# Grouping layer 1's 16-bit and 32-bit products by pairs of block groups

## The chip, the cores and the metric

The kernel runs on one core of a Trainium2 chip. A core has five engines that work side by side, each through its own queue in order: TensorE (PE, matrix products into PSUM), VectorE (DVE), ScalarE (ACT), GpSimd (POOL) and SyncE (SP, which here only issues DMA transfers). The metric is device time in microseconds (us) for one execution, and less is better.

## The reference, cut to what matters

The program is a graph network of four layers over 2708 nodes with 128 features. Its adjacency matrix `adj` is 2708 x 2708, about 0.6% filled plus the diagonal. Every layer normalises its input, applies relu, computes an update and adds it to x. The change touches layer 1 alone, a layer of messages:

```python
s = node_feats @ msg_w[:, :D].T
d = node_feats @ msg_w[:, D:].T
messages = gelu(s[:, None, :] + d[None, :, :] + msg_b)
aggregated = einsum('ijd,ij->id', messages, adj)
new_feats = concatenate([node_feats, aggregated]) @ upd_w.T + upd_b
h = gelu(new_feats) + node_feats          # then a layer norm
```

A message is needed only where `adj[i, j]` is not zero. The kernel therefore lists the non-zero entries of every row first (in layer 0's stage) and computes messages for listed entries only. Layer 0 is a weighted mean over neighbours, layer 2 a gated recurrent cell, layer 3 an attention with two heads.

## The kernel before

**Stages.** From the start of the profiled span to about 215 us the kernel reads `adj`, lists its entries and computes layer 0. Layer 1's set-up runs to about 273 us and its loop from there to 606 us; a tail of small operations follows. Layers 2 and 3 fill the rest.

**Tiles and blocks.** The 2708 rows make 22 tiles of 128 (the last has 20). The columns make 22 blocks of 124 (the last has 104). Six groups of up to four blocks (`GB` = 6) are handled one after another: groups 0 to 4 have four blocks, group 5 has two. For one tile t and one block there are up to 128 listed entries ("slots").

**One period for one tile.** `period(t)` runs for t = 0 to 22. Within it a loop over k = 0 to 5 issues, for the present tile, and for tiles further up and down the pipeline:

- `combine(t, k)` (L620, L624): for each block of group k, six 16-bit (bf16) products into one PSUM tile `p_m`. Three pick the rows' part s (split into three bf16 pieces) by the 0/1 matrix `sel`, three pick the columns' part d by `cols`. This makes s + d for every slot.
- `activate(t, k)` (L632): gelu on ScalarE, from `p_m` to a tile `g` (named `g1`) in SBUF.
- `gather(t, k)` (L645): for each block one 32-bit product of `g` with `put`, which holds the adjacency values at their rows. A 32-bit product shows as two weight loads and two matmuls in the profile (x8 for four blocks). They add up in `agg`. Group k is gathered two steps after it was combined; groups 4 and 5 are gathered in steps 0 and 1 of the next period.
- `close_tile(t - 1)` (L653): the diagonal entries of the tile before are added in 32 bits; after each fourth tile `agg` is copied to `aggT`.
- `pass_on(t + 1)` (L560 to L567): column numbers of the next tile are turned on TensorE (`p_w`), copied out by ScalarE (`where_T`), and sent through DRAM to all partitions (`spread`).
- `rank(t + 3)` (L465 to L467): a 16-bit product `p_r`, and two VectorE copies of it, `ends` and `ends4`.
- `fetch(t + 2, half)` (L498): eleven 16-bit products `y`, and ScalarE copies of them (`lead`, `line`).
- `describe(t + 3)` (L418 to L420, and L474 on POOL): the listed values of a tile split into three bf16 pieces (`xb`), by ScalarE, VectorE, ScalarE and POOL in turn.
- `sources(k)` (L588 to L607), in even periods up to 18: two 32-bit products `p_s` for the next pair of tiles, a VectorE addition (`sb`, L595), and then a split like that of `describe` (`s`, `s_r`), a gelu and two scalings on ScalarE.
- `update(g, 0)` (L679, L680), in periods 5, 9, 13, 17 and 21 inside the loop: eight 32-bit products `p_u` for a group of four tiles, and a VectorE addition. Steps 1 to 7 of `update` follow one period apart each; they are layer 1's gelu, its layer norm and the next layer's norm.
- `select_rows`, `count_rows`, `columns` (L574), `place`, `finish_rows` (L487), `list_late` (L459, L461): VectorE work that prepares `sel`, `cols` and `value` for later tiles. `finish_rows` also waits for a DMA.
- `put_values` (POOL) and `put_more` (ScalarE, L552): make `put`.

**What sets the order.** The loop stands inside `tc.manual_schedule()`. Each engine gets its instructions in the order in which the Python code calls them, and takes them in that order. A tile's buffer can be written again only when the readers of its former content are done. Three pools matter here: `p_m` has two PSUM buffers (`l1m`), `g1` has three buffers (`l1b`), and `p_w`, `p_r`, `p_s` and `p_u` all share the one PSUM bank of `rpool` (tag "r"). So each of these four waits until the one before it has been copied out.

Of the kernel before, what the change touches and what calls it, by code (L numbers as in the profile page):

```python
# [20 lines left out]
F32 = mybir.dt.float32  # L21
# [9 lines left out]
P = 128  # L31
N = 2708
D = 128
# [3 lines left out]
CH = 512  # L37
# [14 lines left out]
def size(t):  # L52
    return min(P, N - t * P)
# [7 lines left out]
def listed_layers(ctx: ExitStack, tc: tile.TileContext, x, adj, w, out, flag):  # L61
# [333 lines left out]
    with (  # L395
# [177 lines left out]
            st["cols"] = work.tile([P, NB, E], BF16, name="cols")  # L573
            nc.vector.tensor_scalar(st["cols"], st.pop("spread"), part, None, ALU.is_equal)  # L574

        own_rows, aggs = {}, {}

        def sources(k):

            p = rpool.tile([P, CH], F32, tag="r", name="p_s")  # L580
            pv = p.rearrange("p (t c d) -> p t c d", t=2, c=2)
            sb = once.tile([P, 2, 2, D], F32, name="sb")
            m = size(2 * k + 1)
            if m < P:
                nc.vector.memset(sb[:, 1, :, :], 0.0)
            for q in range(2):
                c, mq = (2 * k + q) * P, size(2 * k + q)
                nc.tensor.matmul(  # L588
                    p[0:mq, q * 2 * D : (q + 1) * 2 * D], hT[:, c : c + mq],
                    src_self.rearrange("p c d -> p (c d)"), start=True, stop=True,  # L590
                )
            bv = msg_b.unsqueeze(1).to_broadcast([P, 2, D])
            if m == P:
                bv = msg_b.unsqueeze(1).unsqueeze(1).to_broadcast([P, 2, 2, D])
                nc.vector.tensor_tensor(sb, pv, bv, ALU.add)  # L595
            else:
                for q in range(2):
                    mq = size(2 * k + q)
                    nc.vector.tensor_tensor(sb[0:mq, q, :, :], pv[0:mq, q, :, :], bv[0:mq, :, :], ALU.add)
            s3 = three.tile([P, 3, 2, D], BF16, name="s3")  # L600
            rest = once.tile([P, 2, D], F32, name="s_r")
            split([s3[:, q, :, :] for q in range(3)], sb[:, :, 0, :], rest)
            gs = three.tile([P, 2, D], F32, name="gs")
            nc.scalar.activation(gs, sb[:, :, 1, :], AF.Gelu)
            for q in range(2):
                t = 2 * k + q
                nc.scalar.activation(gs[:, q, :], gs[:, q, :], AF.Identity, scale=own[:, t : t + 1])  # L607
            own_rows[k] = s3, gs

        def combine(t, k):  # L610

            st = state[t]
            s3 = own_rows[t // 2][0]
            b0 = 4 * k
            n = min(4, NB - b0)
            p = mpool.tile([P, 4, D], F32, name="p_m")
            for b in range(b0, b0 + n):
                kb = width(b)
                for q in range(3):
                    nc.tensor.matmul(  # L620
                        p[:, b - b0, :], st["sel"][:, b, :], s3[:, q, t % 2, :], start=(q == 0), stop=False
                    )
                for q in range(3):
                    nc.tensor.matmul(  # L624
                        p[:, b - b0, :], st["cols"][0:kb, b, :], d3[0:kb, b, q, :], start=False, stop=(q == 2)
                    )
            st["p", k] = p

        def activate(t, k):
            n = min(4, NB - 4 * k)  # L630
            g = three.tile([P, 4, D], F32, name="g1")
            nc.scalar.activation(g[:, 0:n, :], state[t].pop(("p", k))[:, 0:n, :], AF.Gelu)  # L632
            state[t]["g", k] = g

        def gather(t, k):

            st = state[t]
            m = size(t)
            if k == 0 and t % 4 == 0:
                aggs[t // 4] = acc.tile([P, 4, P], F32, name="agg1")  # L640
            agg = aggs[t // 4][:, t % 4, 0:m]
            g = st.pop(("g", k))
            for b in range(4 * k, min(4 * k + 4, NB)):
                put = (st["put", 0][:, b, 0:m] if b < HP else st["put", 1][:, b - HP, 0:m])
                nc.tensor.matmul(agg, g[:, b - 4 * k, :], put, start=(b == 0), stop=False)  # L645
# [17 lines left out]


        STEPS = 8
        ups = {}

        def update(g, step):
            t, k = GROUPS[g]
            if step == 0:  # L670
                u = work.tile([P, 4, D], F32, name="u1")
                p = rpool.tile([P, CH], F32, tag="r", name="p_u")
                agg = aggs.pop(g)
                if size(t + k - 1) < P:
                    nc.vector.memset(u[:, k - 1, :], 0.0)
                for q in range(k):
                    m, c = size(t + q), (t + q) * P
                    pq = p[0:m, q * D : (q + 1) * D]
                    nc.tensor.matmul(pq, hT[:, c : c + m], upd_wT[:, 0, :], start=True, stop=False)  # L679
                    nc.tensor.matmul(pq, agg[:, q, 0:m], upd_wT[:, 1, :], start=False, stop=True)  # L680
                pv = p.rearrange("p (t d) -> p t d", t=4)
                bv = upd_b.unsqueeze(1).to_broadcast([P, 4, D])
                whole = k if size(t + k - 1) == P else k - 1
                nc.vector.tensor_tensor(u[:, 0:whole, :], pv[:, 0:whole, :], bv[:, 0:whole, :], ALU.add)
                if whole < k:
                    nc.vector.tensor_tensor(u[0:TAIL, whole, :], pv[0:TAIL, whole, :], upd_b[0:TAIL, :], ALU.add)
                ups[g] = [u]
            u = ups[g][0]
            rows = tiles_of(u, 0, k)
            if step == 1:  # L690
                nc.scalar.activation(u[:, 0:k, :], u[:, 0:k, :], AF.Gelu)
            if step == 2:
                nc.vector.tensor_tensor(u[:, 0:k, :], u[:, 0:k, :], h[:, t : t + k, :], ALU.add)
                ups[g].append(moments(rows, "n1u"))
            if step in (3, 6):
                ups[g].append(factors(*ups[g].pop()))
            if step == 4:
                scale_rows(rows, rows, *ups[g].pop(), AF.Identity)
                for v, op in ((ln_w, ALU.mult), (ln_b, ALU.add)):
                    nc.gpsimd.tensor_tensor(u[:, 0:k, :], u[:, 0:k, :], v.unsqueeze(1).to_broadcast([P, k, D]), op)  # L700
            if step == 5:
                nc.vector.tensor_tensor(xs[:, t : t + k, :], xs[:, t : t + k, :], u[:, 0:k, :], ALU.add)
                ups[g].append(moments(tiles_of(xs, t, k), "n2"))
            if step == 7:
                scale_rows(tiles_of(h, t, k), tiles_of(xs, t, k), *ups[g].pop(), AF.Relu)
                ups.pop(g)
# [10 lines left out]
        def period(t, between=()):  # L717

            now, c, b, a = (0 <= t + q < NT for q in range(4))
            last = 0 <= t - 1 < NT  # L720
            if c and not between:
                put_values(t + 1)
            for k in range(GB):
                for step in between[k : k + 1]:
                    step()
                if now:
                    combine(t, k)
                    activate(t, k)
                if k < 2:
                    if last:  # L730
                        gather(t - 1, GB - 2 + k)
                    if k == 0 and c:
                        pass_on(t + 1)
                    if k == 1 and last:
                        close_tile(t - 1)
                    if k == 1 and a:
                        rank(t + 3)
                elif now:
                    gather(t, k - 2)
                if k in (1, 2) and b:  # L740
                    fetch(t + 2, k - 1)
                if k == 1 and a:
                    describe(t + 3)
                if k == 2:
                    if now and t % 2 == 0 and t + 2 < NT:
                        sources(t // 2 + 1)
                    if a:
                        select_rows(t + 3)
                    if now and t + 4 < NT:
                        count_rows(t + 4)  # L750
                    updates(t)
                if k > 0 and c:
                    put_more(t + 1, k)
                if k == 3 and c:
                    columns(t + 1)
                if k == 3 and b:
                    place(t + 2)
                if k == 4 and a:
                    finish_rows(t + 3)
                if k == 4:  # L760
                    load_late(t + 1)
                if k == GB - 1:
                    list_late(t)
# [955 lines left out]
```

## Time and profile before

| What | us |
|---|---|
| Time, median of three runs (lowest to highest) | 1063.65 (1063.14 to 1064.64) |
| The profiled execution's own time | 1064.19 |
| Its span, from the first to the last instruction | 1062.3 |
| Layer 1's loop: first `combine` of tile 0 to last product of `close_tile(21)` | 273.5 to 606.1 |
| PE busy in the whole span | 931.0 (88%) |
| DVE busy | 816.0 (77%) |
| ACT busy | 516.6 (49%) |
| POOL busy | 450.6 (42%) |

The profile is one execution. A page gives busy times, forty slices of the span with busy tenths, and the costliest groups of instructions. The trace behind it answers for any stretch: which instruction ran when, what an engine was idle for, and what ended the idle time. "Period t" below runs from the first product of `combine(t, 0)` to that of `combine(t + 1, 0)`; times "in a period" count from its start. Matmuls overlap in the pipeline, so the distance between two starts is what a matmul costs the engine; its listed duration is longer.

### The profile page before, as it was taken

What the parts mean: (1) busy time and instruction counts of PE and PEld (TensorE: products, weight loads), DVE (VectorE), ACT (ScalarE), POOL (GpSimd) and SP (SyncE); (2) the same over time, 40 slices, a digit from 0 to 9 for tenths busy, and PEclk for the clock granted to TensorE, in tenths of its full rate; (3) what the DMA queues carried; (4) which work ended last, traced back from release to release, by engine and by line L of the source; (5) the groups of instructions that cost most, each with busy time, mean ns of one, the idle gap of its engine ahead of it and who ended that gap; (6) DMA issues with size and microseconds to landing.
All of it is one profiled execution on the core that took longest, in us unless ns stands there. A gap on an engine that the chain in (4) does not pass through costs nothing. (4 is left out here: it accounts for less than half of the span.)

```text
span 1062.3 us, 22020 instructions
## 1 busy us (share of the span) xinstructions
PE 931.0 (88%) x7950; PEld 751.1 (71%) x7950; DVE 816.0 (77%) x2853; ACT 516.6 (49%) x1450; POOL 450.6 (42%) x486
## 2 busy tenths in 40 slices
PE   5798789944799999999999969999979999989983
PEld 2454455433699999899899824444478899989982
DVE  7999999868577788787877264655578977997793
ACT  7777788534666666666666511433312200330142
POOL 3310112022798878787987172344320200250042
PEclk9999999756899999999999979999989999999996
DMA  9889997221233333322321155556410000000000
GB/s 364 312 301 323 308 359 253 74 67 45 80 108 118 125 99 104 106 92 83 108 87 58 65 201 180 199 192 217 124 38 21 12 4 1 2 16 6 1 11 19
DMA packets 60625, 129.67 MB, mean 122 GB/s; under 512 B 11160, under 2 KB 23828, under 8 KB 57798
## 3 DMA queue, kind: packets, MB, share of 16 engines
q1 hardware_dynamic: 58690, 125.38, 34.7%
q10 hardware_dynamic: 1816, 2.80, 0.9%
q8 instruction: 64, 1.05, 0.4%
q14 instruction: 55, 0.45, 0.1%
HBM read 81.55 MB, written 30.87 MB: 106 GB/s over the span
## 5 line engine op out<-in xcount | busy, mean ns | idle before, releaser
L543 POOL TENSOR_SCALAR put<-count,line,value 128x128 f32<-128x128 f32 x176 | 196.3, 1126 | 32.7 <-DVE value L532 24.4
L965 PE MATMUL att<-hv,wt 128*128 128x129 f32 x1672 | 195.5, 278 | 8.8 <-DVE wt L935 8.8
L965 PEld LDWEIGHTS att<-hv,wt 128*128 128x128 f32 x1672 | 191.8, 194 | 11.8 <-DVE wt L935 8.6
L620 PE MATMUL p_m<-s,sel 128*128 128x128 bf16 x1452 | 161.1, 219 | 6.6 <-ACT g L632 6.6
L624 PE MATMUL p_m<-d,cols 124*128 124x128 bf16 (+1 forms) x1452 | 161.4, 219 | 1.4 <-DVE cols L574 1.3
L121 POOL TENSOR_TENSOR n_r<-n_r,minus_half 128x4 f32<-128x4 f32 (+1 forms) x31 | 46.2, 1492 | 269.3 <-DVE n_r L120 263.7
L935 DVE SCALAR_TENSOR_TENSOR wt<-row,lift,mask 128x1024 f32<-128x1024 f32 (+1 forms) x132 | 138.1, 1075 | 25.0 <-PE att L965 25.0
L645 PE MATMUL agg<-put,g 128*128 128x128 f32 (+1 forms) x968 | 135.8, 281 | 0.0
L297 PE MATMUL acc<-a,hs 128*128 128x512 f32 (+2 forms) x264 | 123.9, 572 | 10.9 <-ACT hs L137 10.9
L1104 PE MATMUL p_agg<-a,hs 128*128 128x512 f32 (+2 forms) x264 | 111.7, 566 | 12.1 <-DMA a<-adjT 8.0
L309 PEld LDWEIGHTS p_T<-ident,a 128*128 128x128 f32 x484 | 59.6, 143 | 87.2 <-ACT aT L313 40.0
L645 PEld LDWEIGHTS agg<-put,g 128*128 128x128 f32 x968 | 118.1, 192 | 0.0
L620 PEld LDWEIGHTS <-sel 128*128 128x128 bf16 x1452 | 104.9, 97 | 10.9 <-issue 8.4
L285 DVE FIND_INDEX8 col<-val,a 128x8 uint16<-128x124 f32 (+1 forms) x400 | 106.2, 276 | 0.0
L309 PE MATMUL p_T<-ident,a 128*128 128x128 f32 x484 | 81.7, 287 | 25.3 <-ACT aT L313 19.6
L624 PEld LDWEIGHTS <-cols 124*128 124x128 bf16 (+1 forms) x1452 | 102.1, 97 | 1.9 <-DVE cols L574 1.9
L632 ACT ACTIVATE g<-p_m 128x512 f32<-128x512 f32 x132 | 73.0, 553 | 61.1 <-PE p_m L624 61.1
L552 ACT ACTIVATE put<-mine,value 128x128 f32<-128x128 bf16 x308 | 100.5, 390 | 0.0
L283 DVE MAX8 val<-a 128x8 f32<-128x124 f32 (+1 forms) x400 | 90.6, 266 | 2.8 <-DMA a<-in_adj 2.8
L313 ACT ACTIVATE aT<-p_T 128x512 f32<-128x512 f32 (+2 forms) x132 | 71.1, 541 | 43.9 <-ACT aT L313 33.2
L1104 PEld LDWEIGHTS p_agg<-a,hs 128*128 128x128 f32 (+1 forms) x264 | 48.4, 197 | 62.2 <-issue 52.0
L297 PEld LDWEIGHTS acc<-a,hs 128*128 128x128 f32 (+1 forms) x264 | 44.3, 201 | 26.2 <-issue 15.0
(261 smaller groups left out, 1504.1 us busy)
## 6 DMA issues: line engine op xcount, KB each, us to landing
a<-in_adj SPq DMA_DIRECT2D x21, 1354.0 KB
adjT<-aT SPq DMA_DIRECT2D x105, 256.0 KB
a<-adjT SPq DMA_DIRECT2D x20, 1280.0 KB
spread<-passed SPq DMA_DIRECT2D x22, 704.0 KB
later<-sel SPq DMA_DIRECT2D x22, 616.0 KB
row<-own_d ACTq DMA_DIRECT2D x10, 256.0 KB
later<-sel SPq DMA_DIRECT2D x22, 82.5 KB
adjT<-aT SPq DMA_DIRECT2D x21, 74.0 KB
```

The lines of the kernel that those rows point to most:

```text
L283: nc.vector.max(val[:, n, b, :], block(b))
L285: nc.vector.max_index(col[:, n, b, :], val[:, n, b, :], block(b))
L297: nc.tensor.matmul(accs[ci][:, 0:cw], h[0:m, n, :], sets[n // 4][0:m, n % 4, c : c + cw], start=(n == 0), stop=(n == NT - 1),)
L309: nc.tensor.transpose(p[0:k, q * P : q * P + m], sets[gi][0:m, q, j * P : j * P + k], ident[0:m, 0:m])
L543: nc.gpsimd.tensor_scalar(st["put", 0][:, b, :], count, st["line"][:, b : b + 1], st["value"][:, b : b + 1], ALU.is_equal, ALU.mult,)
L552: nc.scalar.activation(st["put", 1][:, b - HP, :], st["mine"][:, b - HP, :], AF.Identity, scale=st["value"][:, b : b + 1])
L620: nc.tensor.matmul(p[:, b - b0, :], st["sel"][:, b, :], s3[:, q, t % 2, :], start=(q == 0), stop=False)
L624: nc.tensor.matmul(p[:, b - b0, :], st["cols"][0:kb, b, :], d3[0:kb, b, q, :], start=False, stop=(q == 2))
L645: nc.tensor.matmul(agg, g[:, b - 4 * k, :], put, start=(b == 0), stop=False)
L935: nc.vector.scalar_tensor_tensor(wt[:, 0:n], row[:, k, c : c + n], lift[:, j, k : k + 1], mask[:, j, c : c + n], op0=ALU.max, op1=ALU.mult,)
L965: nc.tensor.matmul(banks[s // 3][:, s % 3, :], wt[:, q * P : (q + 1) * P], hv[:, j, k, :], start=(v < 2 and s // 3 not in touched), stop=( ...
L1104: nc.tensor.matmul(pa[:, 0:n], h[0:k, j, :], a[0:k, j - j0, 0:n], start=(j == 0), stop=(j == NT - 1))
```

## The change

Inside `period`, the order of the calls is new. `combine` still runs for k = 0 to 5. The gathers now come two at a time: those of groups 4 and 5 of the tile before in step 1, those of groups 0 and 1 in step 3, those of groups 2 and 3 in step 5. The first of each two stands after `combine(t, k)` and ahead of `activate(t, k)`, the second after `activate(t, k)`. `pass_on` moves ahead of `activate(t, 0)`, and `rank` ahead of both gathers of step 1.

The 32-bit products of `sources` and of `update`'s step 0 are taken out into two new functions, `project` and `mix`, which run in step 1 right after `close_tile`. Before, they stood in step 2. The work that reads them stays in step 2. No instruction is added or removed on any engine.

```diff
+        def project(k):
+
+            p = projected[k] = rpool.tile([P, CH], F32, tag="r", name="p_s")
             for q in range(2):
                 c, mq = (2 * k + q) * P, size(2 * k + q)
                 nc.tensor.matmul(
                     p[0:mq, q * 2 * D : (q + 1) * 2 * D], hT[:, c : c + mq],
                     src_self.rearrange("p c d -> p (c d)"), start=True, stop=True,
                 )
+
+        def sources(k):
+
+            if k not in projected:
+                project(k)
+            pv = projected.pop(k).rearrange("p (t c d) -> p t c d", t=2, c=2)
...
+        def mix(g):
+            t, k = GROUPS[g]
+            p = mixed[g] = rpool.tile([P, CH], F32, tag="r", name="p_u")
+            agg = aggs.pop(g)
+            for q in range(k):
+                m, c = size(t + q), (t + q) * P
+                pq = p[0:m, q * D : (q + 1) * D]
+                nc.tensor.matmul(pq, hT[:, c : c + m], upd_wT[:, 0, :], start=True, stop=False)
+                nc.tensor.matmul(pq, agg[:, q, 0:m], upd_wT[:, 1, :], start=False, stop=True)
...
                 if now:
                     combine(t, k)
+                if k == 0 and c:
+                    pass_on(t + 1)
+                if k == 1 and a:
+                    rank(t + 3)
+                if k == 1 and last:
+                    gather(t - 1, GB - 2)
+                elif k in (3, 5) and now:
+                    gather(t, k - 3)
+                if now:
                     activate(t, k)
-                if k < 2:
-                    if last:
-                        gather(t - 1, GB - 2 + k)
-                    if k == 0 and c:
-                        pass_on(t + 1)
-                    if k == 1 and last:
-                        close_tile(t - 1)
-                    if k == 1 and a:
-                        rank(t + 3)
-                elif now:
+                if k == 1 and last:
+                    gather(t - 1, GB - 1)
+                    close_tile(t - 1)
+                elif k in (3, 5) and now:
                     gather(t, k - 2)
+                if k == 1:
+                    if now and t % 2 == 0 and t + 2 < NT:
+                        project(t // 2 + 1)
+                    for g, (first, n) in enumerate(GROUPS):
+                        if t == first + n + 1:
+                            mix(g)
                 if k in (1, 2) and b:
                     fetch(t + 2, k - 1)
```

## The prediction

> **What bounds the kernel now.** I read the page's busy tenths first, to see which engine carries the stage that changes. Layer 1's loop is slices 10 to 22.
>
> ```profile
> PE   5798789944799999999999969999979999989983
> DVE  7999999868577788787877264655578977997793
> ACT  7777788534666666666666511433312200330142
> PEclk9999999756899999999999979999989999999996
> ```
>
> PE is at 9 and its clock at 9 through the loop, DVE at 7 and 8, ACT at 6. PE sets the pace, with DVE close behind. Next the list of waits, for PE alone, from 291.8 to 603.5 us (periods 1 to 21): whom PE waited for, us in total, times, longest.
>
> ```profile
> PE p_m L620 <- ACT g L632: 5.7, 7, 1.5
> PE y L498 <- DVE sel L487: 2.4, 5, 0.6
> PE p_m L624 <- DVE cols L574: 1.3, 2, 0.6
> ```
>
> So only 9.4 of 312 us are waits, of two kinds. In even periods `combine(t, 5)` waits for `activate(t, 3)`; in odd ones `fetch` or `combine` waits for DVE. Third, PE's timeline in period 8, for what a change of type costs.
>
> ```profile
> 402.05 0.33 PE L624 MATMUL p_m<-d,cols 124*128 124x128 bf16 x3
> 402.21 1.11 PE L645 MATMUL agg<-put,g 128*128 128x128 f32 x8
> 403.16 0.33 PE L620 MATMUL p_m<-s,sel 128*128 128x128 bf16 x3
> ```
>
> Eight 32-bit products hold PE for 0.95 us. Read one by one, the first holds it 0.165 and each other 0.1115; the bf16 ones around take 0.056 each. A bf16-to-f32 change thus costs 0.055 us. The way back costs nothing (0.112 from the last f32 start to the first bf16).
>
> **What the skill says.** The Trainium skill, "TensorE: Matmul & The Clock Gate", section "Weight-path perf modes", says that the fast weight load is off for FP32. The trace agrees: a bf16 load is listed with 96 to 100 ns, an f32 load with 192. The same page, "Architectural detail", says that PE alone pulls weight loads ahead, and that ScalarE and VectorE are strictly first in, first out. The waits above fit that. Its "Part 1: The HAM clock gate" gives free-running windows of 3413 ns, one idle window halving the clock. The record here changes clock at multiples of 3.41 us, and 265.3 to 275.5 us shows half clock released only after a full busy window. "Perfetto Trace Analysis", "Optimization Strategy", says that repeated bubbles can mean that buffers are short. The PSUM bank of `rpool` is such a place below.
>
> **Part 1: fewer changes of type.** Before, a period has 6 runs of f32 products, plus one for `p_s` in 10 even periods and one for `p_u` in 5 odd ones: 6 x 22 + 15 = 147. After, each period has 3, and what is left in period 22 joins the last of them: 66. Saved: 81 x 0.055 = 4.4 us. A period without waits falls from 13.53 us (period 7) to 13.37, an even one from 14.48 to 14.27, one with `mix` from 15.41 to 15.19.
>
> **Part 2: the even periods' chain on ACT.** This is the wait of `combine(t, 5)`. ACT's timeline of period 2 (start 305.33):
>
> ```profile
> 310.26 0.21 ACT L499 CAST lead<-y 128x55 bf16<-128x55 f32 x1 [0.36 <-PE y L498]
> 311.39 0.37 ACT L420 CAST xb<-v_r 128x176 bf16<-128x176 f32 x1 [0.60 <-DVE v_r L419]
> 312.24 0.57 ACT L632 ACTIVATE g<-p_m 128x512 f32<-128x512 f32 x1
> 314.52 0.41 ACT L418 CAST s<-sb 128x256 bf16<-128x256 f32 x1 [1.47 <-DVE sb L595]
> 315.41 0.41 ACT L420 CAST s<-s_r 128x256 bf16<-128x256 f32 x1 [0.49 <-DVE s_r L419]
> 317.65 0.58 ACT L632 ACTIVATE g<-p_m 128x512 f32<-128x512 f32 x1
> ```
>
> The last line is `activate(2, 3)`, 12.32 into the period. The 1.47 us of waiting for `sb` comes from `p_s` standing late in PE's queue. After the change `p_s` is done before `fetch`, so that wait goes. But `fetch` ends at 5.58 instead of 4.74, as `p_s` (0.90) is now ahead of it. From the fetch's end to L418 of `s` ACT has 2.61 us of work (the same lines); then 0.89 to L420 and 2.24 to `activate`, as here: 5.58 + 2.61 + 0.89 + 2.24 = 11.32, 1.0 earlier. But `combine(t, 5)` now also stands one gather (0.89) earlier, so its wait shrinks little. It starts 0.62 after `activate(t, 3)` (as before), and 0.68 + 1.84 (`combine` and two gathers) end the period: 14.46 against 14.57. The same sum for each even period gives 0.1 off, 0.2 off in period 18.
>
> The new wait of the odd `activate` calls for a gather costs nothing: `gather(t, 0)` ends at 10.4 in an even period, ACT gets there at 11.3; `activate(t, 1)` would wait to 3.95 against 3.97 now. What is queued behind, `put_more`, is for the next tile.
>
> DVE waits for the same chain, so its `select_rows` of even periods starts 1.0 earlier. It runs without a gap from there into the odd period, so it comes 0.9 earlier into that. This takes away most of PE's waits for DVE: period 3 falls by 0.75 (0.43 of it wait), periods 11, 15 and 19 by 1.0 each.
>
> **Part 3: the shared bank.** `p_s` and `p_u` now follow `p_r` at once, and have to wait for DVE's `ends` and `ends4`. Before, they stood 2.9 us further on. Without a wait they would now start at 4.40, and they can start 0.38 after `ends` does. The timeline has `ends` at 4.67 in most periods, where DVE was waiting for `p_r` (now 1.65 earlier, so no wait). In periods 5, 8, 9, 12 and 13 it was DVE that was late: 5.26, 4.69, 6.07, 5.54, 4.84. Shifted by what parts 2 and 3 did to the periods before them: 4.36, 4.79, 5.16, 5.65, 3.95; 4.27 in period 14. PE's waits: 0.34, 0.77, 1.14, 1.63, 0 and 0.25. `fetch` and the ACT chain behind them move with these. Period 12 follows from period 11: PE gains 1.0 there, DVE has no gap (it idles 0.6 in 15.1), so PE waits for it one period later.
>
> Period 0 is the worst. DVE's and PE's timelines:
>
> ```profile
> 282.75 0.49 DVE L822 TENSOR_TENSOR d_r<-p_d,d 124x128 f32<-124x128 f32 x2 [6.67 <-POOL d L824]
> 283.15 0.17 DVE L466 CAST ends<-p_r 128x22 bf16<-128x22 f32 x1
> ```
> ```profile
> 283.53 1.13 PE L588 MATMUL p_s<-src_self,hT 128*128 128x256 f32 x4 [1.41 <-DVE ends L467]
> ```
>
> DVE is held by POOL until 282.75, which the change doesn't touch. PE already waits 1.41 here, with 2.9 us of `fetch`, `combine` and `gather` done ahead. After, all that stands behind `p_s`: PE idles from 278.6 to 283.5. Laid out again (`fetch` ends at 284.78, `activate(0, 3)` starts at 290.63), period 0 ends at 293.75 instead of 291.80: 1.95 more. The idle stretch covers the whole clock window from 278.9 to 282.3, so the clock is likely to halve at 282.3. Released at 285.8 this adds 1.1, at 289.2 it adds 2.3; I take 1.75. Its bounds are 0 and 2.3.
>
> **The sum.** More: period 0 3.7, period 5 0.12, period 8 0.68, period 9 0.51, period 12 1.52, period 14 0.14; together 6.7. Less: period 3 0.75; 11, 15 and 19 1.0 each; 1, 2, 4, 6, 7, 10, 16, 18 and 20 to 22 together 1.4; 13 and 17 0.43; together 5.6. Net 1.1 more. After the loop all hangs on the last product of `close_tile(21)` (SP issues layer 2's loads only then, ACT copies `aggT`), so the end moves by the same. Against the profiled execution's 1064.19 that is 1065.3; its time is 0.5 above the median of the runs, so I forecast 1064.8. What a measurement here can tell from no change is about 0.2%, 2.1 us.
>
> POOL and SP have their instructions in the order of before, and the DMAs of `pass_on` start 0.95 us earlier: I cost that at nothing, since only period 20's `cols` waits for that transfer, and PE doesn't wait there.
>
> **Rivals.** *The saving gets through.* If DVE is on time at the bank in periods 5, 8, 9, 12 and 14, they give back 1.15 us in place of costing 3.0, and period 0 costs its 1.95 alone: -5.6 - 1.15 + 1.95 = -4.8, so 1059. For it: DVE idles 5 us in even periods. Against: it hardly does in odd ones, and 11 and 12 show the two in step.
>
> *Slower: the bank waits grow and the old ones stay.* The 0.9 us by which DVE comes earlier hangs on `s_r` (0.42 us in period 2, 1.15 in period 10) and on ACT. If it comes no earlier, PE waits 1.24, 2.05 and 0.82 in periods 5, 9 and 13, 2.6 more than in my sum, and the 3.1 us that I took off periods 3, 11, 15 and 19 for old waits stay: 5.5 more in all, 1070. A fifth of that, DVE 0.2 us later than laid out, is enough for slower by over 0.2%.
>
> *It does not do what it says*: PE is in order, so the runs are joined; I give this nothing.
>
> **How the numbers follow.** My forecast, net within some 2.5 us of 1064.8, has 0.48; its own range is 1062 to 1067.5, with period 0's clock as its largest unknown. The saving that gets through has 0.22, the slower rival 0.30. The range over all is 1059 to 1070. Faster by over 0.2%: 0.23, nearly all from the first rival. Within 0.2%: 0.40. Slower: 0.37, 0.10 of it the upper end of my forecast.
>
> **What would show it.** Runs of 16 f32 products with one start of 0.165 at the head; 0.11 between all others. `p_s` in period 0 waiting some 4.9 us for `ends4`, with a half-clock piece after it. Waits of PE for L467 in periods 5, 8, 9 and 12, longest in 12. Periods 11 and 15 near 14.1 us. Even periods still waiting for `activate(t, 3)`. I am wrong if period 12 is not longer than now (DVE then is no limit), or if periods 2, 4 and 6 differ by more than 0.3 us (the ACT chain is then laid out wrongly).

## The result, and the profile after

The changed kernel took 1064.25 us (median of 14 runs, 1062.0 to 1067.1) beside 1064.39 for the kernel before on the same chip. The ratio is 1.0001, with a 95% interval of 0.9991 to 1.0012: no difference that stands clear of the noise. Two later measurements of the same kernel gave 1.0029 (1.0016 to 1.0042) and 1.0028 (1.0018 to 1.0038), so the change costs between nothing and 0.4% of the time. Its loop is longer in every profile, as shown below.

The profiled execution took 1063.62 us, its span 1061.8. The page's busy tenths of the changed kernel:

```profile
PE   5798889944699999989999969999979999999983
...
DVE  7999999868478777887878164656678987997793
ACT  7777778534566675666666521433322200230142
...
PEclk9999999756699999999999978999999999999996
```

The loop (slices 10 to 22) looks like before: PE at 9, DVE just behind. In slice 10 PE is down to 6 and its clock to 6, where before PE had 7 and the clock 8. That is period 0.

The list of PE's waits in periods 1 to 21 (whom it waited for: us in total, times, longest):

```profile
PE p_m L625 <- ACT g L637: 5.9, 6, 1.7
PE p_s L583 <- DVE ends L467: 1.7, 2, 1.3
PE p_w L560 <- DVE where L531: 1.6, 3, 0.6
PE p_u L680 <- DVE ends L467: 1.3, 1, 1.3
PE p_m L629 <- DVE cols L574: 0.2, 1, 0.2
```

Before, `ends` was not in this list at all. The waits for `sel` (2.4 us) and most of those for `cols` (1.3) are gone; waits at the shared bank (1.7 + 1.3) and for `where` (1.6) stand in their place. The wait of `combine(t, 5)` is as large as it was.

Timeline of PE in period 7, which has no wait (two of its three runs of 32-bit matmuls; lines of `combine` left out):

```profile
387.07 0.43 PE L498 MATMUL y<-xb,sel 128*128 128x37 bf16 x11
...
390.34 2.00 PE L650 MATMUL agg<-put,g 128*128 128x128 f32 x16
...
394.21 2.00 PE L650 MATMUL agg<-put,g 128*128 128x128 f32 x16
```

Sixteen 32-bit matmuls, two for each product, now stand in one run. Read one by one, a run holds PE for 1.839 us, where two runs of eight held it for 2 x 0.945: one change of type costs 0.05. Period 7 fell from 13.53 to 13.41.

All 22 periods, in us, from the first product of `combine(t, 0)` to the next, with the change that the prediction gave:

| Period | Before | After | Difference | Predicted |
|---|---|---|---|---|
| 0 | 18.28 | 22.35 | +4.07 | +3.7 |
| 3 | 14.12 | 13.41 | -0.71 | -0.75 |
| 5 | 15.41 | 15.60 | +0.19 | +0.12 |
| 8 | 15.00 | 15.21 | +0.21 | +0.68 |
| 9 | 15.82 | 16.72 | +0.90 | +0.51 |
| 10 | 15.80 | 15.08 | -0.72 | -0.1 |
| 11 | 15.08 | 14.15 | -0.93 | -1.0 |
| 12 | 16.12 | 17.56 | +1.44 | +1.52 |
| 14 | 15.08 | 15.07 | -0.01 | +0.14 |
| 15 | 15.07 | 14.15 | -0.92 | -1.0 |
| 18 | 15.24 | 15.43 | +0.19 | -0.2 |
| 19 | 14.55 | 14.58 | +0.03 | -1.0 |
| all others | | | -0.98 | -1.5 |
| loop | 332.7 | 335.4 | +2.8 | +1.1 |

The loop here ends with the last product of `close_tile(21)`.

ACT's timeline in period 2 (start 309.66), the chain of the prediction's part 2:

```profile
315.43 0.21 ACT L499 CAST lead<-y 128x55 bf16<-128x55 f32 x1 [1.15 <-PE y L498]
316.48 0.37 ACT L420 CAST xb<-v_r 128x176 bf16<-128x176 f32 x1 [0.51 <-DVE v_r L419]
317.32 0.57 ACT L637 ACTIVATE g<-p_m 128x512 f32<-128x512 f32 x1
317.89 0.41 ACT L418 CAST s<-sb 128x256 bf16<-128x256 f32 x1
318.78 0.41 ACT L420 CAST s<-s_r 128x256 bf16<-128x256 f32 x1 [0.49 <-DVE s_r L419]
321.02 0.58 ACT L637 ACTIVATE g<-p_m 128x512 f32<-128x512 f32 x1
```

The 1.47 us of waiting for `sb` is gone, and `lead` waits longer for `fetch`, which now comes behind `p_s`. `activate(2, 3)`, the last line, starts 11.36 into the period, 0.96 earlier than before. `combine(2, 5)` stands one gather earlier, so the period is 14.50 against 14.57.

Period 0, on DVE and then on PE:

```profile
283.15 0.49 DVE L841 TENSOR_TENSOR d_r<-p_d,d 124x128 f32<-124x128 f32 x2 [6.69 <-POOL d L843]
283.56 0.17 DVE L466 CAST ends<-p_r 128x22 bf16<-128x22 f32 x1
```
```profile
279.00 0.17 PE L465 MATMUL p_r<-rows_n,before 128*128 128x22 bf16 x1 [1.34 <-ACT where_T L562]
283.94 2.08 PE L583 MATMUL p_s<-src_self,hT 128*128 128x256 f32 x4 [4.77 <-DVE ends L467]
```

DVE is late by the same POOL work as before. PE used to spend that time on `fetch`, `combine` and a gather; it now has nothing but `p_s` at the head of its queue.

Period 12 shows the later waits at the bank, again on DVE and then on PE. DVE reaches its copies of `p_r` late, and `p_s` starts when they are done:

```profile
462.73 0.15 DVE L466 CAST ends<-p_r 128x22 bf16<-128x22 f32 x1
462.80 0.23 DVE L467 CAST ends<-p_r 128x88 bf16<-128x88 f32 x1
```
```profile
463.09 1.13 PE L583 MATMUL p_s<-src_self,hT 128*128 128x256 f32 x4 [1.28 <-DVE ends L467]
```

### The profile page after: what moved, and what is told of

The parts are those of the page before. It is cut to its first block, busy times and chain, and to the rows that moved or that the text cites. A ratio compares the mean times of both kernels' runs of the same rounds, so it can differ in the third digit from the quotient of the medians.

```text
span 1061.8 us, 22014 instructions
## 1 busy us (share of the span) xinstructions
PE 928.5 (87%) x7950; PEld 749.4 (71%) x7950; DVE 815.6 (77%) x2853; ACT 513.1 (48%) x1450; POOL 451.5 (43%) x486
## 5 line engine op out<-in xcount | busy, mean ns | idle before, releaser
L650 PE MATMUL agg<-put,g 128*128 128x128 f32 (+1 forms) x968 | 122.5, 278 | 0.0
L650 PEld LDWEIGHTS agg<-put,g 128*128 128x128 f32 x968 | 113.2, 192 | 0.0
```

## The experiments

Each kernel was timed beside the kernel before. "Loop" is as above. Its excess over 332.7 is the more exact measure: the second profile of the kernel before, below, repeats every period to 0.02 us, while the part from layer 2 on, where all kernels have the same code, varies between 445.6 and 449.7 us over 13 profiles, and the loop begins anywhere from 273.3 to 278.9 us into the span.

### Period 0 put back

```diff
-                    if now and t % 2 == 0 and t + 2 < NT:
+                    if now and t > 0 and t % 2 == 0 and t + 2 < NT:
                         project(t // 2 + 1)
```

> The changed kernel, but the p_s of period 0 stays in step 2, as before. Loop = from the first product of combine(0, 0) to the last of close_tile(21): 332.7 us in the kernel before, 335.4 in the changed one. My theory: period 0's wait at the shared bank (4.9 us) and the half clock after it cost some 3.1 us net, and nothing later makes it good. Then period 0 takes about 19.2 us (22.35 changed, 18.28 before), the other periods stay as in the changed kernel to 0.2 us, the loop is 332.3 +- 0.5, and the time about 2 to 3 us below the kernel before. Rival: VectorE sets the pace of the whole loop, so what period 0 gives back is lost again at the bank in periods 5 to 12; then the loop stays at 334.5 or above and the time equals the kernel before.

Measured: period 0 took 19.17, all others as in the changed kernel to 0.1 us but for period 16 (16.78), loop 332.7. Time 1.0008 of the kernel before (0.9999 to 1.0018). The rival falls: periods 8, 9 and 12 are 15.18, 16.72 and 17.54, no longer than when period 0 wasted 3 us. So the two losses, in period 0 and at the bank later, are independent. My expected time was wrong by its own numbers: a loop of 332.3 is 0.4 below the kernel before, not 2 to 3; those are the distance to the changed kernel. Period 0 doesn't fall back to 18.28: the gathers by pairs leave two of them behind its last wait, where there was one. With 0.9 us lost there, the other periods together gain 0.9, and the loop is that of before.

### Pairs only

The call of `project` and `mix` in step 1 is deleted, so both run in step 2.

```diff
-                if k == 1:
-                    if now and t % 2 == 0 and t + 2 < NT:
-                        project(t // 2 + 1)
-                    for g, (first, n) in enumerate(GROUPS):
-                        if t == first + n + 1:
-                            mix(g)
```

> The gathers by pairs, with pass_on and rank moved as in the change, but p_s and p_u left in step 2. My theory: the bank waits of periods 0, 5, 8, 9, 12 and 14 go (ends4 is then read long before), even periods stay at about 14.5 as the ACT chain is as early as in the changed kernel, and 15 more changes of type cost 0.8 us. Loop about 329, period 12 about 16.0 instead of 17.56, time 4 to 6 us below the kernel before (0.4 to 0.6%). Rival: the early p_s was what shortened the even periods and took DVE's lateness away; then even periods are at 15 or above, periods 11 and 15 are back at 15.1, and the time is that of before.

Measured: loop 328.6, time 0.9967 (0.9955 to 0.9979). Periods 5, 8, 9, 11, 12: 15.28, 14.61, 15.28, 14.09, 16.04. PE's two largest waits in the loop:

```profile
PE p_m L625 <- ACT g L637: 5.7, 6, 1.7
PE p_s L583 <- DVE ends L467: 2.6, 1, 2.6
```

One wait of `p_s` at the bank is left, period 0's, and the time is 3.5 us below the kernel before, a little less than expected. The rival, that the early `p_s` was what shortened the even periods, falls: period 2 is 14.49 here and 14.50 in the changed kernel. ACT's chain there (start 307.55):

```profile
315.77 0.41 ACT L418 CAST s<-sb 128x256 bf16<-128x256 f32 x1 [0.78 <-DVE sb L600]
318.90 0.57 ACT L637 ACTIVATE g<-p_m 128x512 f32<-128x512 f32 x1
```

`activate(2, 3)` starts 11.35 into the period, against 11.36 in the changed kernel. `p_s` comes earlier here too, though it stays in step 2, because `gather(t, 0)` no longer stands ahead of it.

### Moves only

`project` and `mix` in step 1, all else in the order of before.

```diff
                 if now:
                     combine(t, k)
-                if k == 0 and c:
-                    pass_on(t + 1)
-                if k == 1 and a:
-                    rank(t + 3)
...
+                if k < 2:
+                    if last:
+                        gather(t - 1, GB - 2 + k)
+                    if k == 0 and c:
+                        pass_on(t + 1)
+                    if k == 1 and last:
+                        close_tile(t - 1)
+                    if k == 1 and a:
+                        rank(t + 3)
...
```

> The other half alone: before's order of gathers, pass_on and rank, but p_s and p_u in step 1 behind p_r. My theory: p_r ends at 4.43 in a period, so ends4 is never read before 5.0, and every period with p_s or p_u waits at least 0.6 us at the bank, those where DVE is late 1.0 to 2.0, period 0 its 4 to 5. Loop 337 to 341, time 4 to 7 us above the kernel before. Rival: the bank waits are made by the pairing (which brings p_r and what follows it forward); then they are no larger than in the changed kernel, and the loop is at 335 or below.

Measured: loop 341.0, time 1.0103 (1.0088 to 1.0118), which is 11 us more and not the 4 to 7 expected. PE's waits at `p_s` and `p_u`:

```profile
PE p_s L583 <- DVE ends L467: 9.2, 10, 4.3
PE p_u L680 <- DVE ends L467: 3.2, 4, 1.6
```

Fourteen bank waits, 12.4 us. The pairing doesn't make them: it brings `p_r` forward and so reduces them to 7.8 (period 0's 4.8 among them). The least of these waits is 0.45 us, not 0.6. ACT's chain in period 2 (start 308.30), where `p_s` waits those 0.45:

```profile
317.48 0.41 ACT L418 CAST s<-sb 128x256 bf16<-128x256 f32 x1
320.61 0.57 ACT L637 ACTIVATE g<-p_m 128x512 f32<-128x512 f32 x1
```

ACT no longer waits for `sb`, yet `activate(2, 3)` starts at 12.31, as in the kernel before (12.32).

### The same order, other banks

```diff
-            p = projected[k] = rpool.tile([P, CH], F32, tag="r", name="p_s")
+            p = projected[k] = bank("p_s")
...
-            p = mixed[g] = rpool.tile([P, CH], F32, tag="r", name="p_u")
+            p = mixed[g] = bank("p_u")
```

> The changed kernel with its order untouched, but p_s and p_u written to the two banks of the pool ps, which the loop does not use otherwise, instead of the bank that p_w and p_r use. My theory: the bank is the cause of all waits at p_s and p_u, so they go: period 0 about 19.2, 5 at 15.2, 8 at 14.5, 9 at 15.2, 12 at 16.0. Loop about 328, time 5 to 7 us below the kernel before. Rival: VectorE is the limit and the bank only the place where it shows; then PE waits for VectorE elsewhere (sel at fetch, cols at combine, where at p_w), and the loop is at 332 or above.

Measured: loop 329.3, time 0.9969 (0.9957 to 0.9981). Periods 0, 5, 8, 9 and 12: 19.22, 15.19, 14.47, 15.20 and 16.01, each as expected to 0.05. The waits that are left:

```profile
PE p_m L625 <- ACT g L637: 10.1, 8, 2.5
PE p_w L560 <- DVE where L531: 1.7, 3, 0.6
PE p_r L465 <- ACT where_T L562: 1.2, 1, 1.2
PE p_m L629 <- DVE cols L574: 0.8, 2, 0.7
```

The shared bank is the cause of the waits at `p_s` and `p_u`: no instruction moved, and they are gone. With no wait at the bank and `p_s` early, `activate(2, 3)` starts at 11.34, no earlier than in "pairs only". The loop is 1.3 us longer than expected and the time 3.3 us below the kernel before, not 5 to 7. Two periods make that up: 14 is at 15.40 and not 15.07, and 11 at 15.10 and not 14.15. In period 11 the rival is right, as PE waits for DVE at `cols` and `where`. DVE is late there mainly because `select_rows` of period 10 took 2.41 us, where the changed kernel has 1.62.

### The kernel before, and the changed one, again

> The kernel before, unchanged, for a second profile beside that of the changed kernel on the same chip. From the first product of layer 2 to the end of the span, in which both kernels have the same code, its first profile shows 449.7 us and those of the changed kernel and of the four experiments show 445.6 to 447.1. My theory: the long one is chance (where the clock's free windows fall), so this profile shows 445 to 448 there, and a loop of 332.7 +- 0.3; the time stands at 1.000 to the kernel before. Rival: the kernel before is really 3 us slower after its loop, and shows 449 to 450 again.

Measured: loop 332.7, from the first product of layer 2 to the end 447.0 us, time 1.0005 (0.9995 to 1.0016). So the 449.7 is no property of the kernel. Whether it was chance or went with the first measurement as a whole is open: the kernel before stood at 1064.39 there and at 1062.05 to 1062.24 in the three later ones.

> The changed kernel, unchanged, for a second profile. My theory: the loop's excess over the kernel before is 0.7 us from the order, and 2.1 more in those executions in which an idle window of the clock falls into period 0's wait. Then this profile shows a period 0 of either 20.2 (clock full, loop 333.3) or 22.35 (clock halved, loop 335.4), the other periods within 0.2 us of the first profile, and the time is 1 to 3 us above the kernel before. Rival: the loop is 335.4 whatever the clock does, and the part after the loop gives 2.7 us back, so that the time is that of before.

Measured: loop 334.4, period 0 22.22, with the half clock; period 19 at 13.62 is the only other that differs by more than 0.2 (14.58 in the first). Time 1.0029 (1.0016 to 1.0042).

> The changed kernel, unchanged, a third time, since its two measurements stand at 1.0001 and 1.0029 to the kernel before. My theory: its loop is 1.7 to 2.8 us longer and nothing after it makes that good, so the time is 1.001 to 1.003 of the kernel before, and period 0 has the half clock again or 20.2. Rival: the first measurement is the true one, the time 0.999 to 1.001.

Measured: loop 336.0, period 0 22.73, period 19 14.58. Time 1.0028 (1.0018 to 1.0038). The half clock was there in all three profiles, and the loop was longer by 2.8, 1.7 and 3.3 us. In two of three measurements the time is longer too, by 3 us, so the rival that nothing is lost doesn't stand for these. The first shows no loss; there the kernel before was 2 us slower than later and the changed kernel 1 us faster (1064.25 against 1065.69 and 1065.39), and why is open.

### The clock kept in period 0

75 products of an identity matrix are added, ahead of `p_s` in period 0. Nothing reads them.

```diff
+                    if t == 0:
+                        idle = bank("p_i")
+                        for _ in range(75):
+                            nc.tensor.matmul(idle[:, 0:E], ident_h, ident_h, start=True, stop=True)
                     if now and t % 2 == 0 and t + 2 < NT:
                         project(t // 2 + 1)
```

> The changed kernel with 75 bf16 products of an identity matrix more, in period 0 ahead of p_s, written to a bank of the pool ps that nothing reads; they fill 4.2 of the 4.9 us that PE waits there. My theory: the wait itself stays, but no clock window is idle, so the clock stays full in period 0: period 0 is 20.2 +- 0.3 instead of 22.35, and the loop 333.3. Rival: the half clock is not caused by the idle window, or costs nothing beside the wait; then period 0 stays at 22.3, or its clock falls all the same.

Measured: period 0 20.09, loop 332.8, time 1.0003 (0.9991 to 1.0016). PE in period 0, by the stretches of 3.41 us at whose ends the clock changes: stretch, its length, PE busy (instructions), the granted clock, DMA share and GB/s. First the changed kernel, then this one:

```profile
279.06:282.47 3.41, 0.11 (x1) 1.00 0.36 97
282.47:285.88 3.41, 1.94 (x5) 0.50 0.30 116
285.88:289.30 3.42, 3.42 (x50) 0.50 0.02 5
289.30:292.71 3.41, 3.41 (x46) 1.00 0.00 0
```
```profile
279.21:282.62 3.41, 3.41 (x64) 1.00 0.55 197
282.62:286.04 3.42, 2.87 (x48) 1.00 0.05 20
286.04:289.45 3.41, 3.41 (x54) 1.00 0.02 5
```

More work makes the loop 2.6 us shorter than in the changed kernel's first profile: with PE kept busy the clock stays full. `p_s` starts 10.0 us into the period in both, so the wait ends no earlier. One all but idle window costs two windows at half clock here, and 22.35 - 20.09 = 2.3 us of period 0. What is left, 20.09 - 18.28 = 1.8, is not the wait alone: period 0 is at 19.2 both with `p_s` back in step 2 and with other banks. So about 0.9 comes from the gathers by pairs, and 0.9 from `p_s` waiting at the bank with `fetch` behind it.

### VectorE's copies ahead of its listing

```diff
                 if k == 1 and a:
                     rank(t + 3)
+                if k == 1 and t > 0:
+                    list_late(t - 1)
...
-                if k == GB - 1:
-                    list_late(t)
```

> The changed kernel with one VectorE call moved: list_late (1.7 us of VectorE per period up to 14) stands behind rank's two copies instead of ahead of them, where VectorE otherwise idles before v_r. Same instructions. My theory: in periods 5, 8, 9 and 12 the bank is held because VectorE reaches ends too late, so with ends some 1.6 us earlier these waits go: period 5 at 15.2, 8 at 14.5, 9 at 15.2 to 15.4, 12 at 16.0. Period 0 keeps its wait (20.2 or 22.3). Loop 331.3 with the half clock in period 0, 329.2 without; time 1 to 3 us below the kernel before. Rival: VectorE's whole work in periods 5 to 12 is the limit, so that what goes at the bank comes back at fetch or at cols; then the sum of periods 5 to 12 stays within 0.5 us of the changed kernel's 122.7.

Measured: periods 5, 8, 9 and 12 at 15.20, 14.78, 16.08 and 16.36; periods 5 to 12 sum to 120.2 against 122.7; loop 333.2; time 1.0009 (0.9998 to 1.0019). The bank waits after period 0 are gone from the list (0.13 us is left in period 9), so it was the place of `ends` in DVE's queue that held the bank. Not all of it is gain: the waits for `where` grew to 2.0 us in four places, among them period 9, and period 21 is at 16.60 (15.92). The rival has its share there. The loop was expected at 331.3, and the time 1 to 3 us below the kernel before; neither came.

### Better versions

> Gathers by pairs, p_u in step 1 as in the change, p_s in step 2 as before, and both in the two banks of ps instead of the shared one. It takes the shorter of the two orders for each: with p_s in step 2 periods 11, 15 and 19 were at 14.1, 14.1 and 13.5, with p_u in step 1 in its own bank periods 5, 9, 13, 17 at 15.2 and 21 at 15.9. My theory: loop 327 to 328.5, time 4 to 6 us below the kernel before (0.4 to 0.6%), as good as the pairs alone or up to 1 us better. Rival: VectorE, which has to wait for the later fetch in the periods with p_u, is late in the periods after; then the loop is at 329 or above, and worse than the pairs alone.

This is the changed kernel with `bank("p_s")` and `bank("p_u")` as above, and with `project` back in step 2:

```diff
-                    if now and t % 2 == 0 and t + 2 < NT:
-                        project(t // 2 + 1)
```

Measured: loop 327.35, time 0.9952 (0.9936 to 0.9968). It is 5 us faster than the kernel before. This is the lowest ratio of all, though the intervals of "pairs only" and "other banks" overlap with it.

> The fastest kernel so far (pairs, p_u in step 1, p_s in step 2, both in the banks of ps) with list_late behind rank's copies too. My theory: little is left for VectorE to hold up, period 11 goes from 14.35 to 14.1 and 14 from 15.34 to 15.0; loop 326.5 to 327.4, time 0.994 to 0.997 of the kernel before. Rival: list_late now delays v_r in the periods where fetch comes early, and even periods grow by 0.3 us or more each; loop 329 or above.

The same, with `list_late` behind `rank`:

```diff
+                if k == 1 and t > 0:
+                    list_late(t - 1)
...
-                if k == GB - 1:
-                    list_late(t)
```

Measured: loop 327.33, time 0.9958 (0.9944 to 0.9971). Periods 11 and 14 stayed at 14.35 and 15.33. `list_late` was no longer in anyone's way.

## Why the prediction was right

The forecast was 1064.8, within 0.2% of before, out of gains and losses that nearly cancel. The time is 1064.25. The loop is longer by 2.8 us in the first profile, and by 1.7 and 3.3 in the others, where the sum had 1.1. So the number came out better than its sum, and that is luck: with the later ratios, 1.0028 and 1.0029, 1063.65 becomes about 1066.7, which is 1.9 above the forecast. That still lies inside the forecast's own range (1062 to 1067.5), but near its end, and is slower by over 0.2%, to which the prediction gave 0.37. What it saw rightly is that gains and losses nearly cancel, and where most of them fall.

**Part 1, changes of type.** Right: 0.055 forecast, 0.05 measured, and runs of 16. A period without waits fell to 13.41 instead of 13.37: the first f32 matmul behind `p_r` holds PE for 0.193 us and not 0.165.

**Part 2, the ACT chain.** Right in size: `activate(2, 3)` at 11.36 against 11.32 forecast, period 2 at 14.50 against 14.46, period 6 at 14.99. The credit went to the wrong move. The prediction lets the wait for `sb` go because `p_s` stands ahead of `fetch`. "Moves only" has that alone and starts `activate(2, 3)` at 12.31, as before, since `fetch` comes later by as much (`lead` at 6.50 into the period instead of 4.93); "pairs only" leaves `p_s` in step 2 and has 11.35. The gathers by pairs bring the microsecond, and the early `p_s` adds nothing to it (11.34 with other banks). The new wait of `activate` for a gather is in the trace, but not on the path. Periods 3, 11 and 15 fell as forecast, and did so in "pairs only" as well. Period 10 fell by 0.72 instead of 0.1, since `s_r` took 0.42 us there and no longer 1.15; that term was taken over from the old profile.

Period 19 is a step that failed: forecast 1.0 shorter, measured 0.03 longer in two of three profiles. The line that I carried forward was `select_rows` of period 18 with 1.62 us. In the first profile of the changed kernel it took 2.41, with a POOL copy beside it that took 1.67. In the second, the same two took 1.62 and 0.47, and period 19 was 13.62, near the forecast. DVE and POOL of the first, then of the second profile:

```profile
560.04 2.41 DVE L437 TENSOR_TENSOR sel<-count_h,ends 128x2816 bf16<-128x2816 bf16 x1
```
```profile
560.93 1.67 POOL L474 COPY xb<-ends 128x22 bf16<-128x22 bf16 x1
```
```profile
564.90 1.62 DVE L437 TENSOR_TENSOR sel<-count_h,ends 128x2816 bf16<-128x2816 bf16 x1
```
```profile
564.65 0.47 POOL L474 COPY xb<-ends 128x22 bf16<-128x22 bf16 x1
```

All 13 profiles agree with this. In six of them the three short POOL operations on `xb` (L421, L473, L474) start while period 18's `select_rows` runs, and it takes 2.40 or 2.41 us. In the other seven they start before or after it, and it takes 1.62 to 1.70. The change made the two meet: `select_rows` starts 9.43 into the period instead of 10.13, and the POOL copy at 10.31 instead of 9.04. The prediction costed POOL at nothing, its instructions being in the order of before; here that failed. That the overlap is what makes both longer is read from these profiles; no run took one of the two away.

**Part 3, the shared bank.** Right: periods 5, 8, 9 and 12 wait 0.14, 0.46, 1.26 and 1.28 us (forecast 0.34, 0.77, 1.14 and 1.63), and other banks remove it. In period 8 I forecast 0.68 more and got 0.21, again by a shorter `s_r`; in period 9 0.51 and got 0.90, as DVE was later relative to the shorter period 8. Period 0 was forecast at 3.7 with the clock's share between 0 and 2.3; it came to 4.07, of which the clock is 2.3, the upper bound, and the rest 1.8, where the laid-out order gave 1.95.

**The rivals.** The saving that gets through (1059) is what other banks give: 0.9969 is 3.3 us below the kernel before. Its condition, no wait at the bank, was the right one. The slower rival (1070) asked that DVE come no earlier; DVE came about as early as laid out. (Its two parts, 2.6 and 3.1, make 5.7 and not 5.5; the end, 1070, stays.)

**After the loop.** "The end moves by the same" holds roughly over the experiments: loops 4.1 and 3.4 us shorter and 8.3 longer gave times about 3.5 and 3.3 us shorter and 11 longer. In the first pair of profiles it doesn't: the span is 0.5 shorter after a loop 2.8 longer. A single profile can't show 3 us here.

## What to carry to other kernels

When instructions of an in-order engine are regrouped, look at what they have to wait for at the new place, not only at what the grouping saves: here the 4 us that the gathers by pairs save in the loop were paid back at one PSUM bank, by products that had been all but harmless 3 us further down the queue, and moving `p_s` up brought nothing of its own. The remedy was the bank, or leaving the two products where they were; both kept most of the saving. And an idle stretch that filled a clock window cost 2.3 us beyond its own length here, so cheap filler work can pay.

## What the runs showed of the hardware

- A 32-bit matmul behind a 16-bit one of 128 columns holds PE about 0.05 us longer than behind another 32-bit one (0.165 against 0.1115); behind a 22-column 16-bit one it is 0.193. The way back costs nothing (0.112 from the last 32-bit start to the first 16-bit one).
- A clock window at half clock with PE busy for 1.94 of 3.41 us did not bring the full clock back; the next one, fully busy, did. A window at full clock need not be idle to lose it: in period 0 of "pairs only" PE was busy for 1.08 of 3.42 us (280.89 to 284.31), and one window at half clock followed; with 2.22 of 3.41 busy the kernel before kept the full clock. Busy time alone sets no border: 1.61 of 3.41 lost the full clock in "moves only" (276.17 to 279.58), and 1.57 kept it in "other banks" (283.49 to 286.90).
- The same VectorE operation took 1.62 or 2.41 us (`select_rows`) and 0.42 or 1.15 us (`s_r`) in the same place of the program, with the same shape. Over the 13 profiles, `s_r` took 0.66 us or more in 11 cases, and in each of them two or three short POOL operations on `xb` started while it ran; in the other 119 it took 0.42 to 0.64.
